# A graph layer's pair work begins five slots behind its split in place of three, with no limit to the tiles planned per slot

## The chip, the core and the metric

The kernel runs on one core of a Trainium2 chip. The core has five engines with instruction streams of their own, each in order: TensorE (PE; its weight loads are listed as PEld), VectorE (DVE), ScalarE (ACT), GpSimd (POOL) and SyncE (SP). They meet through semaphores. DMA transfers run beside them; in this kernel SP issues nearly all plain transfers, and POOL issues the indirect ones.

The metric is the time of one execution on the device in microseconds (us).

## The reference

One message-passing layer over a graph of 6250 nodes and 100000 edges, with rows of 128 numbers, followed by a residual layer norm. The edges come sorted by `dst`.

```python
msg_in = jnp.concatenate([x[src], x[dst], edge_attr], axis=-1)
h = msg_in @ W + b
mu = jnp.mean(h, axis=-1, keepdims=True)
var = jnp.mean(jnp.square(h - mu), axis=-1, keepdims=True)
h = (h - mu) * jax.lax.rsqrt(var + 1e-5) * gamma + beta
msg = jax.nn.relu(h)
out = jax.ops.segment_sum(msg, src, num_segments=6250)
return _layernorm(x + out)
```

## The kernel before

**Two halves and a sort between them.** Edges are taken in 782 tiles of 128, four tiles to a *slot*, 196 slots. The first half of the work handles edges in the order in which they come: `edges(s, q)` (L619, L623) multiplies the four tiles of slot q by the edge part of W and adds, by a product with a one-hot matrix (`edge_hot`, L607), the `dst` node's part from a small window of a node table. `evict` (L633, ACT) copies the result from PSUM to a buffer of the ring `hs`. POOL then scatters each tile's 128 rows to DRAM (L650, `scatters`), to a place that sorts the edges by blocks of `src` nodes. The places are worked out beside this by `places` (L451 to L524, on DVE, PE and ACT), piece by piece, up to about slot 176.

The second half takes the sorted rows back. They lie in *pairs* of node blocks, 25 pairs to a split. `load_pairs` (L725, SP) loads one pair; `ones` (L748, DVE) makes a one-hot matrix of it, `turn` and `turned` (L760 PE, L764 ACT) turn it, `seed` (L770, ACT) and `pick` (L787, PE) add the `src` node's part, `square` (L796, L799, ACT) makes the variance, `root` and `scale` (L805, L811, DVE) normalise, `sums` (L820, PE) sums the messages per node, and `add` (L826, DVE) adds them to the accumulator. The last split is not done by pairs but by `Unit`s at the end, with the final norm.

**Splits.** The edges are cut into six splits that end at slots 42, 84, 126, 156, 176 and 196. A pair of a split can be loaded only when every scatter of that split has landed. A pair of splits 0 to 2 has eight tiles of rows, one of split 3 six, one of split 4 four. In split 4 the first eight *items* hold two pairs each (`TWINS`); all other items hold one pair. There are 117 items.

**The planner.** An item takes four steps; a step runs, in the order of `FLOW`, one stage each of several items, so that items overlap. An item's load stands six steps ahead of its `ones` and twenty ahead of its `add`. The list `due` says at which slot each split's items start and so, by straight lines between, how many steps each slot gets (`steps_due`). In the loop over slots the code of slot q issues, in order: the loads of the edge rows (`eT`, L141), of `db` (L581) and of the window (`win`, L593) for slots up to q + 4; `edges(s, q)`; one step of pair work; `evict(s, q)`; pieces of `places`; the remaining steps; and the scatters of the slot before.

**What holds the streams to each other.** SP is one queue: what stands behind a load that waits is not issued either. The ring `hs` has nine slots' room in three tiles of three slots each; ACT fills the column of block numbers for three slots at once (`fill`, L568, every third slot), and this instruction waits until the scatters of the three slots that had the tile before have landed. Scatters are tied to products on PE (`TIE`), so that POOL spreads them over the next slot.

**Numbers of the planner.** `LAG = 3` starts a split's items three slots behind its end. `MOST = 6.6` keeps the next split from starting before the present one could be done at 6.6 tiles a slot.

Of the kernel before, what the change touches and what calls it, by code (L numbers as in the profile page):

```python
# [22 lines left out]
TILES = 782  # L23
LAST = E - (TILES - 1) * P
NB, BN = 50, 125
RUN = 8
NPAD = 6400
PT = 4
# [9 lines left out]
SPLITS = [(168, 4, 320, [12, 24, 44, 44, 44]),  # L38
          (168, 4, 320, [42, 42, 42, 42]),
          (168, 4, 320, [42, 42, 42, 42]),  # L40
          (120, 3, 192, [40, 40, 40]),
          (80, 2, 128, [40, 40]),
          (78, 2, 128, [39, 39])]
# [15 lines left out]
def first_tiles():  # L59
    out = [0]  # L60
    for n, _, _, _ in SPLITS:
        out.append(out[-1] + n)
    assert out[-1] == TILES
    return out
# [20 lines left out]
def fast_path(ctx, tc, io, bad_d, found):  # L85
# [4 lines left out]
    first_tile = first_tiles()  # L90
# [882 lines left out]
    n_split = len(SPLITS)  # L973
# [95 lines left out]
    TWINS = 8  # L1069
    pairs, first_item = [], []  # L1070
# [50 lines left out]
            n_steps += 1  # L1121

    LEAD, ENDQ, ENDS = 6, 1, 0
    LAG = 3
    MOST = 6.6

    due = []
    for s in range(1, n_split):
        q = first_tile[s] // PT + LAG
        if due:  # L1130
            q = max(q, due[-1][0] + int(NB * SPLITS[s - 2][1] / MOST))
        due.append((q, 4 * first_item[s - 1]))
    q, at0 = due[-1]
    due.append((q + int(4 * TWINS * SPLITS[-2][1] / MOST), at0 + 4 * TWINS))
    due.append((-(-TILES // PT) + ENDQ, len(pairs) * 4 + ENDS))

    def steps_due(q):
# [16 lines left out]
    for s, (n_tiles, _, _, _) in enumerate(SPLITS):  # L1154
        p0, p1 = first_tile[s] // PT, -(-first_tile[s + 1] // PT)
        slots = p1 - p0
        for i in range(slots):
            q = p0 + i
# [140 lines left out]
@with_exitstack  # L1299
def gnn_resnorm_kernel(ctx, tc, io):  # L1300
    nc = tc.nc
    keep = ctx.enter_context(tc.tile_pool(name="keep", bufs=1))
    bad_t = keep.tile([1, 1], I32, name="bad_t")
    with ExitStack() as inner:
        found = []
        fast_path(inner, tc, io, bad_t, found)
    with tc.If(found[0] > 0, preferred_fallthrough_block=True, label="general"):
        with ExitStack() as inner:
            general_path(inner, tc, io)
# [233 lines left out]
```

## Time and profile before

| | |
|---|---|
| runs | 1121.99, 1122.06, 1118.9 us; median 1121.99 |
| the profiled execution | 1117.85 us, its span 1115.9 us |
| PE, DVE busy | 870.6 us (78%), 846.7 us (76%) |
| ACT, POOL busy | 751.9 us (67%), 795.9 us (71%) |
| scatters (L650) | 782 in 757.5 us, from 20.0 to 1023 us |
| DMA | 247.19 MB, 222 GB/s over the span |

An engine's share is an average over very different stretches. A row of the groups gives a line's operation, its count, its busy time and the mean of one, and then the idle time ahead of it with what ended it. A row of the waits names the engine and line that waited, then the one that ended the wait, the sum, the number of waits and the longest. A row of the timeline gives the start, the time taken, the engine, the line, and in brackets the idle time before it with its end. A row of a stretch gives its bounds and length, each engine's busy time with the count of instructions in brackets, then the clock granted to TensorE as a share of full speed, the DMA share and the GB/s; asked for one line, it counts that line alone.

Times in a trace are from the start of the span. The 133rd eviction is slot 132's, since slots count from 0.

### The profile page before, as it was taken

The page shows a single profiled execution, that of the slowest core. Times are in us where ns is not written, and L with a number is a line of the kernel's source. Part 1 is how long each engine was busy: PE and PEld are TensorE (multiplying, and loading weights), DVE is VectorE, ACT ScalarE, POOL GpSimd, SP SyncE. Part 2 cuts the span into 40 slices and gives each one's busy share as a digit, 9 for nine tenths or more (in the row PEclk, how much of TensorE's full clock was granted, in tenths as well). Part 3 has the DMA queues.
Part 4 walks back from the last instruction along what each step waited for, and adds up shares of the span by engine and source line. Part 5 has one row for each costly group of instructions (what it writes and reads, how often), then busy time and mean ns, then how long its engine had stood idle before and what let it go on. Part 6 is the DMA issues. An engine that isn't in the chain of part 4 may idle for free. (4 is left out here: it accounts for less than half of the span.)

```text
span 1115.9 us, 27253 instructions
## 1 busy us (share of the span) xinstructions
PE 870.6 (78%) x8886; PEld 805.4 (72%) x8886; DVE 846.7 (76%) x2368; ACT 751.9 (67%) x2980; POOL 795.9 (71%) x830
## 2 busy tenths in 40 slices
PE   6748755456878888598968678988989899987994
PEld 4647645456867887587868668888878788886773
DVE  8784556628769586688877668889898988877897
ACT  4324422126666667577777657898888899987895
POOL 2777777777777777777777777777777767774254
PEclk7879878668989788898989897999999999999998
DMA  7899999458777763877867648787778767844341
GB/s 216 262 267 272 283 311 284 150 182 286 230 228 253 234 205 126 270 231 245 274 223 242 186 134 281 244 253 241 230 245 259 226 209 241 262 136 141 105 134 61
DMA packets 128049, 247.19 MB, mean 222 GB/s; under 512 B 47005, under 2 KB 61231, under 8 KB 127897
## 3 DMA queue, kind: packets, MB, share of 16 engines
q1 hardware_dynamic: 101924, 191.92, 56.9%
q0 software_dynamic: 25104, 53.05, 13.2%
q8 instruction: 71, 1.16, 0.5%
q14 instruction: 80, 0.66, 0.2%
q10 hardware_dynamic: 870, 0.40, 0.1%
HBM read 155.49 MB, written 89.80 MB: 220 GB/s over the span
## 5 line engine op out<-in xcount | busy, mean ns | idle before, releaser
L650 POOL DMA_INDIRECT sorted<-hs,place_i x782 | 757.5, 969 | 249.8 <-issue 100.9
L787 PE MATMUL sel<-xa,ohn 128*128 128x128 bf16 x2550 | 188.9, 226 | 83.7 <-ACT sel L770 82.0
L619 PEld LDWEIGHTS hp<-w,eT 128*128 128x128 f32 x1564 | 216.4, 212 | 48.7 <-issue 30.2
L820 PE MATMUL pa<-msg,ohe 128*128 128x130 f32 x1700 | 236.6, 292 | 17.1 <-DVE acc L826 8.6
L619 PE MATMUL hp<-w,eT 128*128 128x128 f32 x1564 | 237.7, 300 | 14.1 <-ACT hs L633 14.1
L811 DVE SCALAR_TENSOR_TENSOR msg<-sel,rstd,cut 128x128 f32<-128x128 f32 x850 | 240.6, 345 | 8.0
L796 ACT ACTIVATE sq<-sel 128x128 f32<-128x128 f32 x850 | 223.7, 282 | 23.1 <-PE sel L787 23.1
L787 PEld LDWEIGHTS <-ohn 128*128 128x128 bf16 x2550 | 165.7, 101 | 94.3 <-issue 80.2
L820 PEld LDWEIGHTS pa<-msg,ohe 128*128 128x128 f32 x1700 | 213.9, 201 | 23.2 <-DVE acc L826 10.4
L796 ACT ACTIVATION_READ_ACCUMULATOR sq<-sel 128x1 f32 x850 | 180.9, 213 | 0.0
L748 DVE TENSOR_TENSOR ohe<-hl,beside 128x1024 f32<-128x1024 f32 (+2 forms) x117 | 130.2, 1113 | 57.2 <-DMA hl<-sorted 41.1
L633 ACT COPY hs<-hp 128x512 f32<-128x512 f32 x196 | 113.2, 579 | 59.1 <-PE hp L623 56.7
L770 ACT COPY sel<-hl 128x512 f32<-128x512 f32 (+1 forms) x225 | 128.1, 569 | 33.0 <-DVE msg L811 32.7
L764 ACT COPY ohn<-tr 128x1024 bf16<-128x1024 bf16 (+2 forms) x117 | 107.7, 921 | 5.3 <-PE tr L760 5.3
L607 DVE TENSOR_SCALAR ohd<-db,part_w 128x512 bf16<-128x512 bf16 x192 | 70.4, 367 | 51.7 <-DMA db<-drel_d 48.6
L568 ACT COPY hs<-sloc 128x12 f32<-128x12 f32 x66 | 14.1, 213 | 132.9 <-DMA sorted<-hs,place_i 131.1
L826 DVE TENSOR_TENSOR acc<-acc,pa 128x260 f32<-128x260 f32 x125 | 52.3, 418 | 57.6 <-PE pa L820 56.7
L760 PE MATMUL tr<-ident_h,ohe 128*128 128x128 bf16 x850 | 70.5, 227 | 26.8 <-DVE ohe L748 14.9
L623 PE MATMUL hp<-win,ohd 126*128 126x128 bf16 x782 | 80.8, 228 | 2.3 <-DMA win<-xb_d 2.3
L805 DVE RECIPROCAL rstd<-std 128x4 f32<-128x4 f32 (+1 forms) x225 | 38.1, 169 | 57.7 <-ACT std L799 56.0
L760 PEld LDWEIGHTS <-ohe 128*128 128x128 bf16 x850 | 55.6, 102 | 28.0 <-DVE ohe L748 16.1
L799 ACT ACTIVATE std<-ss,eps 128x4 f32<-128x4 f32 (+1 forms) x225 | 66.9, 297 | 7.3
(198 smaller groups left out, 1039.3 us busy)
## 6 DMA issues: line engine op xcount, KB each, us to landing
eT<-in_eT SPq DMA_DIRECT2D x96, 512.0 KB
hl<-sorted SPq DMA_DIRECT2D x75, 528.0 KB
db<-drel_d SPq DMA_DIRECT2D x96, 256.0 KB
sorted<-empty SPq DMA_DIRECT2D x100, 198.0 KB
hl<-sorted SPq DMA_DIRECT2D x50, 264.0 KB
sorted<-hs,place_i POOLq DMA_INDIRECT x782
hl<-sorted SPq DMA_DIRECT2D x25, 396.0 KB
sorted<-empty SPq DMA_DIRECT2D x50, 132.0 KB
```

The lines of the kernel that those rows point to most:

```text
L619: pe(nc.tensor.matmul(hp[:, j, :], eT[:, at], w[:, 2, :], start=j == 0, stop=False, skip_group_check=True), 4)
L623: pe(nc.tensor.matmul(hp[:, j, :], oh[:3 * WN, at], win[:3 * WN, :], start=False, stop=j == m - 1, skip_group_check=True))
L633: nc.scalar.copy(hs[:, :m, 0:D], hp[:, :m, :])
L650: i = nc.gpsimd.indirect_dma_start(out=sorted_d[s][:, :], out_offset=bass.IndirectOffsetOnAxis(ap=place_i[:parts, t:t + 1], axis=0), in_=h ...
L748: nc.vector.tensor_tensor(self.ohe[:, :k, :], self.hl[:, :k, D:D + 1].to_broadcast([P, k, P]), row_bc(iota_p, k), op=ALU.is_equal)
L760: pe(nc.tensor.transpose(tr[:, j, :], half[:, j0 + j, 1::2], ident_h))
L764: nc.scalar.copy(self.ohn[:, :self.k, :], self.tr[:, :self.k, :])
L770: nc.scalar.copy(self.sel[g][:, :m, :], self.hl[:, j0:j0 + m, 0:D])
L787: pe(nc.tensor.matmul(sel[:, j, :], self.ohn[:, j0 + j, :], xa[:, b, i * D:(i + 1) * D], start=False, stop=j == m - 1 and i == 2, skip_gro ...
L796: nc.scalar.activation(sq[:, j, :], self.sel[g][:, j, :], AF.Square, accum_out=ss[:, j:j + 1])
L811: nc.vector.scalar_tensor_tensor(self.msg[:, j0 + j, 0:D], self.sel[g][:, j, :], rstd[:, j:j + 1], cut, op0=ALU.mult, op1=ALU.max)
L820: pe(nc.tensor.matmul(self.pa[:, h, :], self.ohe[:, i * k + j, :], self.msg[:, i * k + j, :], start=(j == h), stop=(j == k - 2 + h)), 4)
```

## The change

`LAG` becomes 5, `MOST` goes, and the start of a split's items no longer looks at the split before. The date at which the two-pair items end is reckoned by another formula.

```diff
     LEAD, ENDQ, ENDS = 6, 1, 0
-    LAG = 3
-    MOST = 6.6
-
-    due = []
-    for s in range(1, n_split):
-        q = first_tile[s] // PT + LAG
-        if due:
-            q = max(q, due[-1][0] + int(NB * SPLITS[s - 2][1] / MOST))
-        due.append((q, 4 * first_item[s - 1]))
+    LAG = 5
+
+    due = [(first_tile[s] // PT + LAG, 4 * first_item[s - 1]) for s in range(1, n_split)]
     q, at0 = due[-1]
-    due.append((q + int(4 * TWINS * SPLITS[-2][1] / MOST), at0 + 4 * TWINS))
+    due.append((q + (TILES // PT + ENDQ - q) * 2 * TWINS // (NB // 2), at0 + 4 * TWINS))
     due.append((-(-TILES // PT) + ENDQ, len(pairs) * 4 + ENDS))
```

Worked out, the list of dates is this (slot at which the items begin):

| items of | steps counted there | before | after |
|---|---|---|---|
| split 0 | 0 | 45 | 47 |
| split 1 | 100 | 87 | 89 |
| split 2 | 200 | 129 | 131 |
| split 3 | 300 | 159 | 161 |
| split 4, two-pair items | 400 | 181 | 181 |
| split 4, single items | 432 | 190 | 190 |
| end | 468 | 197 | 197 |

Splits 0, 1 and 2 have the same number of slots as before (42, 42, 30). Split 3 has 20 in place of 22: five steps a slot for 4.5, and 25 pairs of six tiles in 20 slots are 7.5 tiles a slot for 6.8. In the list of before the limit moved one date, split 4's, from 179 to 181.

ACT at the boundary of split 2, before: the rows around `fill` of slot 132 (L568, `hs2_195`). `hl_8429` is the last pair of split 1, `hl_8566` the first of split 2.

```order
L770 COPY sel_8793<-hl_8429 128x512
L796 ACTIVATE sq_8796,ss_8795<-sel_8752 128x128 x4
L799 ACTIVATE std_8801<-ss_8795,eps_100 128x4
L764 COPY ohn_8775<-tr_8776 128x1024
L568 COPY hs2_195<-sloc_164 128x12
L633 COPY hs2_195<-hp_8819 128x4x128
L770 COPY sel_8867<-hl_8566 128x512
```

The same place in the changed kernel; `hl_8373` and `hl_8492` are the last two pairs of split 1.

```order
L568 COPY hs2_195<-sloc_164 128x12
L633 COPY hs2_195<-hp_8672 128x4x128
L770 COPY sel_8746<-hl_8373 128x512
L796 ACTIVATE sq_8749,ss_8748<-sel_8696 128x128 x4
L799 ACTIVATE std_8754<-ss_8748,eps_100 128x4
L764 COPY ohn_8728<-tr_8729 128x1024
L633 COPY hs2_195<-hp_8768 128x4x128
L477 ACTIVATE sc_8465<-sc_8465 128x1000
L770 COPY sel_8813<-hl_8492 128x512
```

Before, split 1's last pair is seeded ahead of slot 132's `fill`, and the first pair of split 2 follows the eviction; now the last two pairs of split 1 are still seeded behind that `fill` and two evictions, and split 2's first pair comes two slots later. On SP, 134 window loads stand ahead of the first load of split 2 before, and 136 now.

ACT in slot 167, in the stage of split 3, from its eviction to the `fill` of slot 168, before:

```order
L633 COPY hs_194<-hp 128x4x128
L770 COPY sel<-hl 128x384
L796 ACTIVATE sq,ss<-sel 128x128 x3
L799 ACTIVATE std<-ss,eps 128x3
L764 COPY ohn<-tr 128x768
L770 COPY sel<-hl 128x384
L796 ACTIVATE sq,ss<-sel 128x128 x3
L799 ACTIVATE std<-ss,eps 128x3
L568 COPY hs_195<-sloc 128x12
```

And in the changed kernel:

```order
L633 COPY hs_194<-hp 128x4x128
L770 COPY sel<-hl 128x384
L796 ACTIVATE sq,ss<-sel 128x128 x3
L799 ACTIVATE std<-ss,eps 128x3
L770 COPY sel<-hl 128x384
L796 ACTIVATE sq,ss<-sel 128x128 x3
L799 ACTIVATE std<-ss,eps 128x3
L764 COPY ohn<-tr 128x768
L770 COPY sel<-hl 128x384
L796 ACTIVATE sq,ss<-sel 128x128 x3
L799 ACTIVATE std<-ss,eps 128x3
L568 COPY hs_195<-sloc 128x12
```

One more group of seed, squares and root stands between the two evictions.

## The prediction

> **What bounds the kernel now.** I read the groups of the page first, then the waits of ACT and of SP's queue, then the timeline where the longest waits stand, and last a ledger by stage. The groups and waits:
>
> ```profile
> L650 POOL DMA_INDIRECT sorted<-hs,place_i x782 | 757.5, 969 | 249.8 <-issue 100.9
> ACT hs L568 <- DMA sorted<-hs,place_i: 131.1, 27, 11.1
> ```
>
> POOL issues one scatter after the other, with 0.3 us between them, and ACT waits 27 times, 131.1 us in all, for a buffer of the ring `hs` that POOL has not yet emptied: over much of the program POOL sets the pace. Whether it does so everywhere is told by counting evictions (L633, one a slot), scatters (L650) and finished pairs (L826) in the same stretches:
>
> ```profile
> 236.50:660.00 423.50, 48.45 (x84) 0.89 0.72 228
> 236.50:660.00 423.50, 322.23 (x333) 0.89 0.72 228
> 0.00:676.50 676.50, 77.05 (x133) 0.85 0.75 234
> 676.50:820.30 143.80, 15.58 (x27) 0.98 0.77 243
> 826.50:918.50 92.00, 9.24 (x16) 1.00 0.75 230
> 676.50:820.30 143.80, 109.33 (x114) 0.98 0.77 243
> 826.50:918.50 92.00, 66.06 (x69) 1.00 0.75 230
> ```
>
> (Each row: the stretch, its length, busy time and count, then clock, DMA share and GB/s. Rows 1, 3, 4 and 5 are evictions, rows 2, 6 and 7 scatters.) From 236.5 to 660 us, 84 slots take 423.5 us, 5.04 a slot, and 333 scatters take 1.27 us each, four of them 5.09: POOL's pace. From 676.5 to 820.3 a slot takes 143.8/27 = 5.33, more than POOL needs, and from 826.5 to 918.5 it takes 92/16 = 5.75. There POOL runs dry: 69 scatters at 1.27 are 87.6 of 92 us, so 4.4 us are lost. So from the eviction of slot 132 (the 133rd, in at 676.5) the other engines are the bound, and they are evenly full:
>
> ```profile
> 676.50:820.30 143.80, 128.12 (x1491) 122.86 (x1490) 125.77 (x356) 125.15 (x515) 109.33 (x114) 0.98 0.77 243
> 826.50:918.50 92.00, 80.72 (x936) 76.19 (x934) 81.56 (x241) 82.69 (x348) 66.06 (x69) 1.00 0.75 230
> 918.50:942.50 24.00, 22.30 (x265) 21.25 (x265) 20.86 (x71) 23.39 (x102) 18.21 (x20) 1.00 0.76 236
> ```
>
> PE, DVE and ACT stand at 87 to 90% in the first two rows (PE, its weight loads, DVE, ACT, POOL). What comes ahead of 676.5 is a stall, where split 2's first pair is loaded (waits of SP's queue, then timeline rows of SP, DVE, ACT and PE):
>
> ```profile
> SPq L725 <- DMA sorted<-hs,place_i: 30.0, 1, 30.0
> SPq L725 <- DMA sorted<-hs,place_i: 18.0, 1, 18.0
> SPq L725 <- DMA sorted<-hs,place_i: 19.1, 1, 19.1
> SPq L725 <- DMA sorted<-hs,place_i: 3.4, 1, 3.4
> 664.17 0.34 SPq L725 DMA_DIRECT2D hl<-sorted  x1
> 668.27 1.22 DVE L748 TENSOR_TENSOR ohe<-hl,beside 128x1024 f32<-128x1024 f32 x1 [7.81 <-DMA hl<-sorted]
> 672.96 0.59 ACT L770 COPY sel<-hl 128x512 f32<-128x512 f32 x1 [10.74 <-DVE msg L811]
> 675.85 0.59 ACT L633 COPY hs<-hp 128x512 f32<-128x512 f32 x1
> 669.55 1.03 PE L760 MATMUL tr<-ident_h,ohe 128*128 128x128 bf16 x8 [7.50 <-DVE ohe L748]
> ```
>
> The four waits are the ends of splits 0 to 3. At the third the load leaves at 664.17, when the last scatter of slot 125 has landed; DVE stands for 7.81 us, PE 7.50, ACT 10.74. After the first two stalls the slots are light enough to make the loss good at POOL's pace; after the third they never do, as every slot costs more than 5.09.
>
> **The change part by part.** Due times of splits 0 to 3 move two slots later; 181, 190 and 197 stay. Nothing is added or removed: 117 items, 782 scatters, the same loads.
>
> *Splits 0 and 1.* Evictions wait for POOL there and POOL keeps its 5.09 a slot throughout, stalls of 30.0 and 18.0 us included. Cost zero, hidden by POOL's backlog; without it each later pair would cost its whole time.
>
> *The third boundary.* The same loads and edges now stand two slots further on when SP comes to the first load of split 2: 136 window loads are ahead of it in place of 134. The release stays at 664.17, since POOL sets it. Two estimates give the moment that answers to 676.4, the end of slot 132's eviction, which is now the end of slot 134's. From the load: 676.4 again, at most, as DVE's first `ohe` can begin at 668.27. From the ring: slot 132's buffer (L568, every third slot) wants slots 123 to 125 landed, the same event, so its eviction ends about 664.2 + 0.6 = 664.8, and two slots at 5.33 make 675.5. I take 676.0, with -1 and +2 as ends: **-0.4 us**.
>
> *From there to slot 181.* Before: 143.8 to slot 159, 6.2 to slot 160, 92.0 to slot 176, 24.0 to slot 181, in all 266.0 us for 49 slots; the finished pairs in them are
>
> ```profile
> 676.50:820.30 143.80, 9.59 (x23) 0.98 0.77 243
> 820.30:826.50 6.20, 0.41 (x1) 1.00 0.97 317
> 826.50:918.50 92.00, 7.49 (x18) 1.00 0.75 230
> 918.50:942.50 24.00, 2.50 (x6) 1.00 0.76 236
> ```
>
> 48. After: the same 48 in 47 slots. So two slots of edges without pairs leave the bounded stretch. PE's part of one is these rows, 1.11 + 0.39 = 1.50 us:
>
> ```profile
> 681.70 1.11 PE L619 MATMUL hp<-w,eT 128*128 128x128 f32 x8
> 682.64 0.39 PE L623 MATMUL hp<-win,ohd 126*128 126x128 bf16 x4
> 88.60:104.20 15.60, 3.58 (x6) 1.00 0.92 278
> ```
>
> At the 88% to which PE is filled that is 1.7 us a slot, so **-3.4 us** for two. Below: ACT's eviction alone (0.58 us at 90%), 1.3 for two. Above: the quickest run of slots without pairs, six evictions in 15.6 us (last row), 2.6 a slot, 5.2 for two.
>
> *The denser stage.* Split 3's 25 pairs take 20 slots in place of 22: 7.5 tiles a slot for 6.8, five steps a slot for 4.5. If time goes by work, slots 161 to 181 take 266.0 - 143.8 - 3.4 = 118.8 us, 5.94 each, against 5.09 for POOL. The lead over POOL pays for that. At its own pace POOL lands slot 161 at 664.2 + 36 x 5.09 = 847.4; the slot is evicted at 676.0 + 143.8 = 819.8, so the lead is 27.6 us. Before, slot 160 led by only 842.4 - 826.5 = 15.9 when POOL began to run dry. At 5.94 - 5.09 = 0.85 a slot, 20 slots eat 17 us, and POOL runs dry in the last few slots before 181 at most. Cost beyond the ledger: zero, if no engine waits longer per step; it is the thinnest part.
>
> *From slot 181.* Same due times, same items, same units behind; PE, DVE and ACT bring their gain along, and POOL, which no longer loses the 4.4 us, comes as early.
>
> Sum: -0.4 - 3.4 = **-3.8 us**. The profiled execution took 1117.85 us with a span of 1115.9; that becomes 1114.0 and 1112.1. The median of the runs, 1121.99, lies 4.1 above the profiled execution, so I forecast 1118.2 for a median.
>
> *The clock.* A stall also halves PE's clock; the same 16 products before and after the stall, and a short wait at slot 123:
>
> ```profile
> 653.83 2.00 PE L820 MATMUL pa<-msg,ohe 128*128 128x130 f32 x16
> 676.38 3.82 PE L820 MATMUL pa<-msg,ohe 128*128 128x130 f32 x16
> 620.77 0.21 ACT L568 COPY hs<-sloc 128x12 f32<-128x12 f32 x1 [5.39 <-DMA sorted<-hs,place_i]
> 622.91 1.22 PE L787 MATMUL sel<-xa,ohn 128*128 128x128 bf16 x12 [2.63 <-ACT sel L770]
> 624.78 1.98 PE L619 MATMUL hp<-w,eT 128*128 128x128 f32 x8
> 664.00:668.00 4.00, 0.00 (x0) 0.00 (x0) 0.00 (x0) 0.00 (x0) 2.95 (x4) 0.52 0.73 194
> ```
>
> After the long stall L820 costs 1.8 us more; after a wait of 2.63 us L619 still costs 0.9 more (1.98 for 1.11). The change swaps a long stall for a wait on the ring like that at 620.77, so the halving stays, only shorter. The Trainium skill, TensorE: Matmul & The Clock Gate, section HAM oscillation — how this bites in real kernels, says that gaps over about 3.4 us throttle the array again. By it a wait of 2.63 us should cost nothing, and the change would save the whole slow stretch; the trace shows slow products behind that wait, so the row decides here. I leave this term out of the sum and make it a rival.
>
> **The rivals.**
>
> (a) *The dense stage gets slower steps.* Place: slots 161 to 181, DVE and ACT. For it: both are at 89 and 90% in the row of 826.5, and a fifth step in a slot finds no slack. Against it: ACT reaches 39.68 of 41.0 us (97%) at the two-pair items:
>
> ```profile
> 942.50:983.50 41.00, 36.74 (x438) 35.54 (x438) 32.62 (x98) 39.68 (x169) 31.25 (x33) 1.00 0.81 255
> 840.00:860.00 20.00, 17.57 (x205) 16.55 (x205) 15.87 (x50) 17.37 (x73) 14.51 (x15) 1.00 0.76 239
> ```
>
> It decides from (942.4 - 819.8)/20 = 6.13 us a slot: above that slot 181 is later than before, and POOL dry for it. If DVE is held at the 79% of its worst 20 us (second row) in place of 89%, 118.8 becomes 133.8, 11 us later than before; half way, 6.5 a slot, is +7: **1129**.
>
> (b) *The ring takes the stall's place.* Slot 135 wants the buffers of slots 126 to 128, so evictions can meet the ring's end there and at slot 138, and the two slots gained are waited away. For it: the 131.1 us of L568. Against: slot 128 has landed at 664.2 + 3 x 5.09 = 679.4, and slot 135 comes at 676.0 + 5.3 = 681.3. Then the gain is 0 to 1: **1121.5**.
>
> (c) *The clock comes back too.* L820 1.8 us, L787 1.2, L619 0.9 and the rest of the slow stretch to 681 are about 4.6 us, against 1.8 behind a short wait; were all 2.8 on the path, **1115.4**.
>
> (d) That the change does nothing it says is out: the orders differ at every boundary. Only the limit on tiles is nearly idle: it held back split 4 alone, and its new date is the same 181.
>
> **How the numbers follow.** Forecast 0.45, its own range 1115.5 to 1120; (a) 0.30, (b) 0.13, (c) 0.12. A measurement of this kernel tells about 0.3%, 3.4 us, from no change. The forecast is barely past that: 0.33 of its 0.45 faster, 0.12 same. (c) is faster, (b) same, (a) slower but for 0.04. Faster 0.45, same 0.29, slower 0.26. The range leaves out 0.1 at each end: above most of (a), below a gain of both ledger ends with the clock: 1111 to 1128.
>
> **What would show it.** At the third boundary SP's wait of 19.1 us falls to about 9, and DVE's of 7.81 to under 3; ACT's total at L568 grows by 10 us or more. Slot 134 is evicted at 676, slot 161 near 820, slot 181 near 938.6; POOL's scatters from 826.5 to 918.5 are 72, not 69. Wrong: slots 161 to 181 take over 122 us (a); evictions 135 to 140 wait at L568 (b); or everything holds to 181 and the gain is lost behind it, which I have no row for.

## The result, and the profile after

Over 17 runs each, taken in turn on the same chips, the changed kernel has a median of 1116.76 us (1114.78 to 1119.06) and the kernel before 1119.7 us (1117.3 to 1123.26). The ratio is 0.9967, with a 95% interval of 0.9959 to 0.9976: 3.7 us of 1120, or 0.33%.

The runs of one kernel spread over some 5 us, more than the effect. The profiled execution of before, at 1117.85, is one of its quicker ones; that of the changed kernel, at 1116.76, is its median. So the two traces show how the time is spent, but their ends lie only 1.0 us apart (spans 1115.9 and 1114.9).

SP's waits at the ends of splits 0 to 3 in the changed kernel:

```profile
SPq L725 <- DMA sorted<-hs,place_i: 18.6, 1, 18.6
SPq L725 <- DMA sorted<-hs,place_i: 13.0, 1, 13.0
SPq L725 <- DMA sorted<-hs,place_i: 14.2, 1, 14.2
SPq L725 <- DMA sorted<-hs,place_i: 3.8, 1, 3.8
```

The first three were 30.0, 18.0 and 19.1. At the third, DVE, which had stood for 7.81 us, now stands for 2.46 (timeline of DVE):

```profile
669.87 1.22 DVE L748 TENSOR_TENSOR ohe<-hl,beside 128x1024 f32<-128x1024 f32 x1 [2.46 <-DMA hl<-sorted]
```

The load itself left at 665.85 us, where it had left at 664.17 (timeline of SP):

```profile
665.85 0.34 SPq L725 DMA_DIRECT2D hl<-sorted  x1
```

What stands in the stall's place is the ring (timeline of ACT, then of PE, then ACT's waits over the whole program):

```profile
653.12 0.21 ACT L568 COPY hs<-sloc 128x12 f32<-128x12 f32 x1 [4.06 <-DMA sorted<-hs,place_i]
665.82 0.21 ACT L568 COPY hs<-sloc 128x12 f32<-128x12 f32 x1 [0.74 <-DMA sorted<-hs,place_i]
```

```profile
654.35 1.25 PE L787 MATMUL sel<-xa,ohn 128*128 128x128 bf16 x12 [3.29 <-ACT sel L770]
655.39 3.27 PE L820 MATMUL pa<-msg,ohe 128*128 128x130 f32 x16
662.78 2.00 PE L820 MATMUL pa<-msg,ohe 128*128 128x130 f32 x16
668.63 2.01 PE L820 MATMUL pa<-msg,ohe 128*128 128x130 f32 x16
```

```profile
ACT hs L568 <- DMA sorted<-hs,place_i: 157.0, 33, 14.9
```

ACT waits 4.06 us at slot 129's fill and 0.74 at slot 132's; from 640 to 690 us it waits there 6.6 us in all, and in the kernel before not at all. PE's products are slow from 654 to 658.5 and at full pace after that, where before they were slow from 669.5 to 681.

The stages behind the boundary, cut at the evictions of slots 134, 161 and 181 (first evictions, L633, then finished pairs, L826, then all engines: PE, its weight loads, DVE, ACT, POOL):

```profile
0.00:677.80 677.80, 78.19 (x135) 0.85 0.75 235
677.80:823.40 145.60, 15.64 (x27) 0.98 0.77 246
823.40:941.30 117.90, 11.55 (x20) 1.00 0.71 229
```

```profile
677.80:823.40 145.60, 9.57 (x23) 0.98 0.77 246
823.40:941.30 117.90, 10.41 (x25) 1.00 0.71 229
```

```profile
677.80:823.40 145.60, 127.04 (x1472) 121.40 (x1472) 127.40 (x356) 124.68 (x514) 110.85 (x115) 0.98 0.77 246
823.40:941.30 117.90, 105.01 (x1235) 99.57 (x1232) 104.79 (x320) 109.83 (x469) 88.24 (x92) 1.00 0.71 229
```

Slot 134 is evicted at 677.8, where the kernel before had done slot 132 at 676.5. So the evictions are further ahead of POOL, and this distance is called the lead from here on: the time from the end of a slot's eviction to the start of its last scatter. At slot 134 it is 707.7 - 687.9 = 19.8 us before and 708.1 - 677.7 = 30.4 after, at slot 161 10.9 and 22.6. Slots 161 to 181 cost 117.9/20 = 5.90 us each with five steps in each; ACT is the fullest there, with 109.83/117.9 = 93%.

POOL's scatters from 826.5 to 941.5 us, the stretch of split 3, in the kernel before and in the changed one:

```profile
826.50:941.50 115.00, 83.57 (x87) 1.00 0.76 232
```

```profile
826.50:941.50 115.00, 86.05 (x89) 1.00 0.71 229
```

At 1.27 us a scatter POOL could issue 115/1.27 = 90.5; where it issues fewer it stands *dry*, without a slot to scatter. The first and the last scatter's start, before and after:

```profile
L650 POOL DMA_INDIRECT sorted<-hs,place_i x782: 868/967/1178, 20.0 to 1022.9; - x196
```

```profile
L650 POOL DMA_INDIRECT sorted<-hs,place_i x782: 867/967/1482, 19.6 to 1021.7; - x196
```

From the last scatter's start to the end it is 1115.9 - 1022.9 = 93.0 and 1114.9 - 1021.7 = 93.2 us. This is the reading that orders the runs below: in eight of the eleven profiles of the next table this tail is 93.0 to 93.4 us. There a kernel's time is the moment of POOL's last scatter plus the tail, and that moment is POOL's own pace plus what POOL stands dry: 782 scatters begin 781 steps apart, 781 x 1.272 = 993.4 us, and before it is 20.0 + 993.4 + 9.5 us of standing dry.

### The profile page after: what moved, and what is told of

Its sections match the earlier page's. It is cut to its first block, busy times and chain, and to the rows that moved or that the text cites. A ratio compares the mean times of both kernels' runs of the same rounds, so it can differ in the third digit from the quotient of the medians.

```text
span 1114.9 us, 27250 instructions
## 1 busy us (share of the span) xinstructions
PE 872.9 (78%) x8886; PEld 807.9 (72%) x8886; DVE 845.3 (76%) x2368; ACT 752.4 (67%) x2980; POOL 797.5 (72%) x830
## 5 line engine op out<-in xcount | busy, mean ns | idle before, releaser
L619 PE MATMUL hp<-w,eT 128*128 128x128 f32 x1564 | 240.5, 303 | 20.8 <-ACT hs L633 20.8
L796 ACT ACTIVATE sq<-sel 128x128 f32<-128x128 f32 x850 | 223.6, 282 | 30.6 <-PE sel L787 30.4
L820 PE MATMUL pa<-msg,ohe 128*128 128x130 f32 x1700 | 231.8, 289 | 15.3 <-DVE acc L826 8.6
L820 PEld LDWEIGHTS pa<-msg,ohe 128*128 128x128 f32 x1700 | 211.4, 200 | 19.8 <-DVE acc L826 10.3
L748 DVE TENSOR_TENSOR ohe<-hl,beside 128x1024 f32<-128x1024 f32 (+2 forms) x117 | 130.2, 1113 | 21.9 <-DMA hl<-sorted 11.6
L633 ACT COPY hs<-hp 128x512 f32<-128x512 f32 x196 | 113.3, 579 | 42.8 <-PE hp L623 40.1
L770 ACT COPY sel<-hl 128x512 f32<-128x512 f32 (+1 forms) x225 | 128.1, 570 | 13.6 <-DVE msg L811 13.2
L568 ACT COPY hs<-sloc 128x12 f32<-128x12 f32 x66 | 14.1, 213 | 159.8 <-DMA sorted<-hs,place_i 157.0
L826 DVE TENSOR_TENSOR acc<-acc,pa 128x260 f32<-128x260 f32 x125 | 52.3, 418 | 58.8 <-PE pa L820 58.7
L623 PEld LDWEIGHTS <-ohd 126*128 126x128 bf16 x782 | 66.4, 105 | 6.0 <-issue 2.4
```

The lines of the kernel that those rows point to most:

```text
L619: pe(nc.tensor.matmul(hp[:, j, :], eT[:, at], w[:, 2, :], start=j == 0, stop=False, skip_group_check=True), 4)
L623: pe(nc.tensor.matmul(hp[:, j, :], oh[:3 * WN, at], win[:3 * WN, :], start=False, stop=j == m - 1, skip_group_check=True))
L633: nc.scalar.copy(hs[:, :m, 0:D], hp[:, :m, :])
L748: nc.vector.tensor_tensor(self.ohe[:, :k, :], self.hl[:, :k, D:D + 1].to_broadcast([P, k, P]), row_bc(iota_p, k), op=ALU.is_equal)
L770: nc.scalar.copy(self.sel[g][:, :m, :], self.hl[:, j0:j0 + m, 0:D])
L796: nc.scalar.activation(sq[:, j, :], self.sel[g][:, j, :], AF.Square, accum_out=ss[:, j:j + 1])
```

## The experiments

Each kernel was timed beside the kernel before, on the same chip. Three kernels that were timed on a chip where every kernel is slower are left out of this table; they come below. The ratios, and what the profiles show. The last two columns are worked out from the starts of the scatters in each trace: what the time from the first scatter of slot 160 to the first of slot 181 exceeds 84 x 1.272 us, and the time from there to the last scatter 57 x 1.272:

| kernel | ratio to before, 95% interval | last scatter begins | span | tail | scatters in 826.5 to 941.5 | dry, slots 160 to 180 | dry, from 181 |
|---|---|---|---|---|---|---|---|
| before | 1 | 1022.9 | 1115.9 | 93.0 | 87 | 5.3 | 1.9 |
| changed | 0.9967 (0.9959 to 0.9976) | 1021.7 | 1114.9 | 93.2 | 89 | 2.0 | 3.3 |
| late_third | 0.9964 (0.9952 to 0.9976) | 1020.1 | 1113.1 | 93.0 | 90 | 0.7 | 3.3 |
| late_first_two | 1.0007 (0.9995 to 1.0019) | 1025.8 | 1118.9 | 93.1 | 85 | 7.8 | 1.9 |
| only_split2 | 0.9959 (0.9945 to 0.9973) | 1023.3 | 1117.4 | 94.1 | 89 | 3.0 | 1.9 |
| no_limit | 1.0069 (1.0056 to 1.0083) | 1031.5 | 1126.8 | 95.3 | 80 | 14.7 | 0.0 |
| lag5_limit | 0.9963 (0.9948 to 0.9979) | 1016.1 | 1113.7 | 97.6 | 91 | 0.2 | 0.2 |
| lag7 | 1.0087 (1.0065 to 1.0109) | 1035.3 | 1128.4 | 93.1 | 86 | 7.1 | 12.4 |
| dense18_b | 1.0073 (1.0055 to 1.0092) | 1032.9 | 1126.1 | 93.2 | 83 | 12.4 | 3.4 |
| ring12_lag5 | 0.9950 (0.9934 to 0.9966) | 1017.5 | 1110.9 | 93.4 | 91 | 0.0 | 2.8 |
| ring12_lag8 | 0.9952 (0.9936 to 0.9968) | 1019.5 | 1112.7 | 93.2 | 90 | 0.3 | 1.6 |

(only_split2's profiled execution, 1119.18 us, is the slowest of its five; its median is 1116.39. POOL stood dry for 4.3 us in its first 44 slots, where its dates are those of the kernel before, which lost 1.6 there.)

The runs of one kernel differ by as much as the effect, as that one shows, but the dry time from slot 160 on goes with the date of split 2's boundary. With 131 it is 5.3, 4.0 and 4.9 us (changed, late_third, only_split2), with 129 it is 7.2 and 9.7 (before, late_first_two). The means are 3.7 us apart, as much as the ratio.

### Which boundary carries the gain

late_third moves the dates of splits 2 and 3 alone, late_first_two those of splits 0 and 1 alone, only_split2 that of split 2 alone:

```diff
-    due = [(first_tile[s] // PT + LAG, 4 * first_item[s - 1]) for s in range(1, n_split)]
+    due = [(first_tile[s] // PT + LAG[s], 4 * first_item[s - 1]) for s in range(1, n_split)]
 # late_third
+    LAG = {1: 3, 2: 3, 3: 5, 4: 5, 5: 5}
 # late_first_two
+    LAG = {1: 5, 2: 5, 3: 3, 4: 3, 5: 5}
 # only_split2
+    LAG = {1: 3, 2: 3, 3: 5, 4: 3, 5: 5}
```

> Splits 2 and 3 begin five slots behind their end, as in the changed kernel (131, 161), splits 0 and 1 three, as before (45, 87); split 4 at 181. Stall theory (two slots of edges move out of the bounded stretch at the boundary of split 2): the whole gain, a ratio to before of 0.9965 to 0.9975, SP's wait there 10 to 15 us, and slot 134 evicted near 677 us. Early theory (the gain comes from the boundaries of splits 0 and 1): 1.000. Chance theory (it comes from how the steps of the places meet those of the pairs, which any shift stirs up): anywhere from 0.995 to 1.003.

> Splits 0 and 1 begin five slots behind their end (47, 89), splits 2 and 3 three, as before (129, 159); split 4 at 181. Stall theory: no gain, 0.9995 to 1.001, as the stall of 19 us on SP at split 2's boundary stays and POOL hides the other two. Early theory: the whole gain, 0.9967.

> Only split 2 begins two slots later (131); split 3 stays at 159, so split 2's items have 28 slots in place of 30, 7.1 tiles a slot, and split 3's 22. Stall theory: the whole gain again, 0.9965 to 0.9975, since the work behind the stall is the same in another order. Lead theory (it takes split 3's later start too, since the edges must stay ahead of POOL): half of it or less, 0.998 to 1.000.

Measured: 0.9964, 1.0007 and 0.9959. In late_third SP's wait there is 12.1 us and slot 134 is evicted at 676.7, both as the stall theory had it. The whole gain sits at split 2's boundary, and one date, 129 to 131, is enough for it. The early theory falls: with splits 0 and 1 moved the interval holds 1 and not 0.9967. The chance theory is not needed: three kernels that share the one date, and differ in the others, agree within their intervals, and the one without it has none of the gain. The lead theory, which asked for split 3's later start too, falls as well.

### The limit alone

```diff
-    LAG = 5
+    LAG = 3
```

> Three slots behind, as before, with the limit on tiles taken away alone: the dates are 45, 87, 129, 159 and then 179 for split 4 (181 before), 189 for its single items. Stall theory: nothing, 0.999 to 1.001; the stall at split 2 is as before, and the work behind it is the same in all. If the denser split 3 (20 slots) costs time in itself: slower, 1.002 or more.

Measured: 1.0069, so slower by 0.7% where I had expected nothing. The limit's formula for the two-pair items goes with it, which moves the single items from 190 to 189. Split 3 is as dense as in the changed kernel, five steps a slot, but the evictions have not gained on POOL at split 2's boundary: at slot 134 the lead is 708.6 - 688.6 = 20.0 us, as before. POOL's row over the same stretch as above:

```profile
826.50:941.50 115.00, 76.30 (x80) 0.99 0.70 224
```

80 scatters in place of 87, so 7 x 1.27 = 9 us more in which POOL stands dry, and its last scatter begins 8.6 us later (1031.5 for 1022.9). The pairs that were done early there bring nothing back, for the end waits for POOL. So taking the limit away costs 0.7% at three slots, while with five slots the pair of edits gains 0.3%.

### The later start with the limit kept

```diff
-    LAG = 3
+    LAG = 5
```

(made in the kernel before, so that the dates are 47, 89, 131, 161, 183, 192)

> Five slots behind, but the limit of 6.6 tiles a slot and its formulas kept: dates 47, 89, 131, 161, then 183 for split 4 (the limit binds: 161 + 22) and 192 for its single items, which have five slots in place of seven. Lead theory (a stage may be dense only while the evictions are far ahead of POOL's scatters; POOL's lost time is not made good): split 3 is a little lighter, but the single items' 36 steps in five slots, 7.2 a slot, come when the lead is gone, so POOL runs dry at slots 192 to 196 by 5 us or more: 0.999 to 1.003. Theory that the limit does nothing once the boundary is at five slots: 0.9967 as the changed kernel.

Measured: 0.9963. The first theory's number was wrong. POOL is not dry at the end: split 3 in 22 slots keeps enough of the lead to carry the single items.

```profile
826.50:941.50 115.00, 87.55 (x91) 1.00 0.76 235
941.50:1016.50 75.00, 57.02 (x60) 1.00 0.59 181
```

Both rows are at full pace (115/91 = 1.26, 75/60 = 1.25), and the last scatter begins 5.6 us sooner than in the changed kernel. Yet the time is the same: the tail grows from 93.2 to 97.6 us, since more work is left when POOL is through: PE is busy for 79.99 us from 1017 to 1113, and in the changed kernel for 76.33 from 1022 to 1114. With five slots, then, taking the limit away costs nothing that these runs can tell (0.9967 beside 0.9963); it only moves work between these two places.

### Seven slots

```diff
-    LAG = 5
+    LAG = 7
```

> Seven slots behind in place of five: dates 49, 91, 133, 163, 181. Ring theory (evictions can be at most about seven to nine slots ahead of POOL, so two further slots of edges can't be put into the stall; ACT waits at the ring in their place, and split 3 has 18 slots, 8.3 tiles each): no better than five, 0.997 to 1.002, with SP's wait at split 2's boundary gone and ACT's total at the ring's fill above 170 us. Stall theory without a ring: another 3 us, 0.994.

Measured: 1.0087. The expectation has the dates wrong: seven slots move split 4 as well, to 183, so split 3 keeps 20 slots and the two-pair items and the single items are pressed into eight and six slots. The trace shows both parts. At split 2's boundary the load finds its rows all but landed (SP's waits) and ACT waits at the ring (ACT's waits, both between the boundary's bounds of 640 and 690 us; 179.7 in all):

```profile
SPq L725 <- DMA sorted<-hs,place_i: 1.1, 1, 1.1
```

```profile
ACT hs L568 <- DMA sorted<-hs,place_i: 13.5, 3, 7.3
```

And POOL issues 61 scatters from 945 to 1035 us, where 90/1.27 = 71 were possible:

```profile
945.00:1035.00 90.00, 58.76 (x61) 1.00 0.58 175
```

So the ring theory's direction holds, that two further slots bring nothing, but its price was read from the wrong dates. The last scatter begins 13.6 us later than in the changed kernel. POOL stands dry for 5.1 us more in slots 160 to 180, and for 9.1 us more from slot 181 on, where the items are pressed. So the larger part is the end's; how much of the other the ring at the boundary costs is open.

### Density with a lead

Split 3 in 18 slots, all else as in the changed kernel:

```diff
-    LAG = 5
+    LAG = {1: 5, 2: 5, 3: 5, 4: 7, 5: 5}
```

> Dates 47, 89, 131, then 163 for split 3 (161 in the changed kernel), 181: split 2 has 32 slots, split 3 only 18, 8.3 tiles a slot. Lead theory (a dense stage costs nothing while the evictions lead POOL by more than the stage eats; the time is POOL's last scatter plus 92 us): the lead at slot 163 is larger than before by what split 2 saves, the work up to slot 181 is the same, POOL dry for 1 to 4 us between slots 160 and 182: 0.996 to 0.998. Theory that density costs time in itself: 0.999 or more.

On that chip every kernel took about 1350 us, the one before included: 0.9987 (0.9965 to 1.0009). In this trace POOL has gaps of up to 3.6 us for no reason that the trace names, so nothing of the kernel's own balance can be read there. The same kernel on a chip of the usual speed:

> The same kernel as dense18 once more (dates 47, 89, 131, 163, 181; split 3 in 18 slots, 8.3 tiles a slot), since that job ran where all kernels, the one before included, took 1350 us. Lead theory: 0.996 to 0.998, POOL dry for 1 to 4 us between slots 160 and 182, last scatter plus 92 us. Theory that density costs time in itself: 0.999 or more.

Measured: 1.0073. The lead theory's number was wrong. Evictions, then finished pairs, from the eviction of slot 134 to those of slots 161 and 181:

```profile
677.90:823.80 145.90, 15.56 (x27) 0.96 0.77 245
823.80:952.50 128.70, 11.58 (x20) 0.98 0.69 212
```

```profile
677.90:823.80 145.90, 8.75 (x21) 0.96 0.77 245
823.80:952.50 128.70, 11.27 (x27) 0.98 0.69 212
```

The first stretch has 21 pairs in place of 23 and takes 145.9 us in place of 145.6: by these two traces, lighter slots are not quicker there. Of the time that should have been saved 1.5 us went into a longer wait at the ring (3.3 us for 1.8), and the granted clock was 0.96 for 0.98; the rest is not explained. The engines are less full in it (all engines of this kernel; DVE 123.02 of 145.9, 84%, where the changed kernel has 127.40 of 145.6, 87%):

```profile
677.90:823.80 145.90, 122.16 (x1390) 117.44 (x1389) 123.02 (x339) 118.08 (x483) 110.82 (x116) 0.96 0.77 245
823.80:952.50 128.70, 114.97 (x1323) 109.30 (x1322) 111.31 (x337) 117.61 (x501) 88.80 (x92) 0.98 0.69 212
```

So no lead is gained by putting two pairs off (23.1 us at slot 161, for 22.6), and the two pairs cost 128.7 - 117.9 = 10.8 us in the next stage. POOL stands dry for 12.4 us there in place of 2.0. This is the price of density: not per step (128.7/27 = 4.8 us a pair against 117.9/25 = 4.7), but as slots that run longer than POOL's four scatters and eat the lead.

### A larger ring

Twelve slots in `hs` in place of nine. To make room `w3`, `iota_row`, `sgn` and `b_bc` go to the pool that closes at slot 44, and the scratch tile of the squares has one buffer (the diff leaves out the four moved tiles, and two further places like that of `sq`):

```diff
-    HS, HG = 9, 3
+    HS, HG = 12, 3
-            sq = blk.tile([P, PT, P], F32, name="sq")
+            sq = blk.tile([P, PT, P], F32, name="sq", bufs=1)
 # ring12_lag8, beside this
+    LAG = {1: 8, 2: 8, 3: 8, 4: 8, 5: 5}
```

> The ring has twelve slots in place of nine (some early tiles go to the pool that closes at slot 44, and the scratch of the squares has one buffer in place of two, to make room), and splits 0 to 3 begin eight slots behind: 50, 92, 134, 164; split 4 at 181. Ring theory: three more slots of edges go ahead of split 2's boundary, 3 x 1.7 = 5 us less behind it, POOL never runs dry up to slot 181: 0.991 to 0.994, lead at slot 137 above 35 us. Theory that five slots is the best for another reason (a later split 3 is too dense: 17 slots, 8.8 tiles each): 0.997 or more.

> The ring of twelve slots alone, dates as in the changed kernel. Ring theory: the order of work is that of the changed kernel, and at split 2's boundary the load is waited for again in place of the ring: 0.996 to 0.998. If the ring's waits cost time by themselves anywhere else (ACT waits 157 us there in the changed kernel): 0.994 or less.

> The ring of twelve slots with the dates of the kernel before (three slots, limit kept). Queue theory (at three slots it is SP, stopped at the first load of a split with the edges' loads behind it, that holds the edges, not the ring): the stall of split 2 keeps its place in the program, so nothing is gained there; 0.9985 to 1.0005. Ring theory alone (more buffers, more lead): 0.995 as with five slots.

> The ring of twelve slots and six slots behind for splits 0 to 3 (48, 90, 132, 162), split 4 at 181. If the time is POOL's last scatter plus 92 us, and POOL is dry for only some 5 us of the whole run with the twelve slots and five: the floor is near, 0.993 to 0.995, at best 2 us under that kernel. If the moved edges count in full (1.7 us a slot): 0.9935.

Measured: 0.9952 with eight slots, 0.9950 with five; each ratio lies between the numbers of its two theories, so neither number held. ring12_lag3 and ring12_lag6 were timed only on the chip on which every kernel took 1350 us (0.9998, 0.9972 to 1.0025; and 0.9972, 0.9948 to 0.9996) and tell nothing of this balance. In the kernel before ACT does not wait at the ring at all from 640 to 690 us; whether a larger ring would help at three slots is left open all the same. With twelve slots and five behind, the wait for the load is back (waits between 640 and 690, ring12_lag5):

```profile
DVE ohe L748 <- DMA hl<-sorted: 17.8, 1, 17.8
```

and still the kernel is no slower for it: POOL's backlog hides the stall (the lead at slot 134 is 31.4 us), POOL keeps its pace through split 3 (91 scatters, dry for 0.0 us), and the tail is 93.4. Three more slots of edges in that stall (ring12_lag8) buy nothing further: the lead at slot 161 grows from 25.4 to 38.1 us, but POOL was not dry before slot 181 any more, so there was nothing left to save there. My 5 us for them did not come. ring12_lag5 has the lowest median of all, 1114.71 us, and is quicker than the kernel before; from the changed kernel its interval does not separate it.

## Why the prediction was right, and where its steps were not

**What bounds the kernel.** Right, and it reaches further than I put it. From slot 132 the other engines are slower than POOL, and from about slot 160, when the lead is eaten, POOL runs dry; and because most of these kernels end 93 us after POOL's last scatter, dry time there is what the kernel pays. no_limit and dense18_b show it with the sign turned round.

**Splits 0 and 1 at zero.** Right: late_first_two, 1.0007.

**The third boundary, -0.4.** Slot 134 came at 677.8, not 676.0: +1.3 against the 676.5 of before, inside the ends of -1 and +2. The step that was off is "The release stays at 664.17": the load left at 665.85, 1.7 us later. In the traces of eight of these kernels it left between 664.02 and 666.96, so the figure of one trace was taken for a fixed one. From the release to the eviction it is 11.9 us, for 12.3 before: 0.4 less, as forecast. The ring bound where I had put it, at slot 132 (0.74 us), and also at slot 129 (4.06 us), where I had not. The load bound less: DVE stood 2.46 us for it, and in late_third, only_split2 and lag5_limit not at all.

**The work behind it, -3.4.** The sum nearly held: 145.6 + 117.9 = 263.5 us against 262.6 forecast and 266.0 before, so 2.5 us were saved. Its ground did not quite. I priced two slots of edges by PE's share, as if time went by work. dense18_b shows a stretch in which two pairs less save nothing, so 1.7 us a slot is not shown as the price of an edge slot, and 2.5 for 3.4 may be chance. Shown is that the date at split 2's boundary alone brings the whole 0.3 to 0.4%.

**The size.** -3.8 us forecast. By the ratio it is -3.7; by the two profiles slot 181 came at 941.3 for 942.5, 1.2 us sooner and not 3.8. The profile of before is a quick one of its kernel, which is part of that difference; how much of it, one trace of each cannot say. That the two sizes agree to 0.1 us is luck: the interval alone goes from 2.7 to 4.6 us, and the terms were off in both directions. One was missing, too: I had POOL lose next to nothing any more. It still lost 2.0 us in slots 160 to 180 (5.3 before), and from slot 181 on it lost more, 3.3 for 1.9. As a time, 1118.2 was forecast and 1116.76 measured; the kernel before, from which it was reckoned, had a median of 1121.99 in three runs and of 1119.7 in 17.

**The denser stage and rival (a).** 118.8 us forecast for slots 161 to 181, 117.9 measured; 5.90 us a slot, under the 6.13 from which (a) would have decided. The lead that was to pay for it was smaller than I had it: slot 161 was evicted at 823.4, not 819.8, which takes 3.6 us off the 27.6. The rival's price is real all the same: at 128.7/20 = 6.4 a slot the median of dense18_b is 1128.46 beside 1120.96, 7.5 us more, where I had priced (a) at +7 for 6.5 a slot. That price was not what I called it: half way between 118.8 and 133.8 us are 6.3 a slot and +4 us, not 6.5 and +7. And the rival's mechanism, slower steps, is not what dense18_b shows: DVE does not fall to 79% (it is at 111.31/128.7 = 86%), a pair costs 4.8 us for 4.7, and there are more steps in each slot than the lead can pay for.

**Rival (d) and the limit.** Here a sentence was wrong: "Only the limit on tiles is nearly idle". It moved split 4's date by two slots, and with its formula the single items' by one, and that is worth 0.7% as long as the start is at three.

**Rival (b).** The ring did take part of the stall's place, with 4.8 us at slots 129 and 132, but at slots 135 and 138, where I had put it, next to nothing: one wait of 1.8 us in all from 677.8 to 823.4. ACT's total at L568 went from 131.1 to 157.0, more than the 10 us that I had named as a sign, but only 6.6 of these 25.9 us lie at split 2's boundary; the others come earlier, so the total is no sign of what happens there.

**The clock and rival (c).** I said that the halving stays, only shorter. So it was: four microseconds behind the ring's wait in place of twelve. L820 took 3.27 us in place of 2.00 behind a gap of 3.29, at a granted clock of 0.82 from 652 to 656 us and 0.75 from 656 to 660. By the page of the Trainium skill on the clock gate (TensorE: Matmul & The Clock Gate, section HAM oscillation — how this bites in real kernels) a gap has to exceed about 3.4 us. The trace shows that a gap just under that is enough, and the 2.63 us of the kernel before were too; the measurement decides. How much of the gain is the clock's was not tried alone.

**The signs.** Scatters from 826.5 to 918.5 were 71, where I forecast 72 and before had 69 (POOL of the changed kernel):

```profile
826.50:918.50 92.00, 68.92 (x71) 1.00 0.71 229
```

SP's third wait fell to 14.2, not to 9: 1.7 us of that are the later release, and SP came to the load of split 2 some 3.5 us sooner than I had reckoned from the evictions. In late_third it fell to 12.1, in only_split2 to 9.7. DVE's wait fell to 2.46, under the 3 forecast.

## What to carry to other kernels

When one engine's queue sets the end, ask of every edit what it does to the lead over that queue: work put into a wait lengthens the lead, a dense stage eats it, and what the queue stands dry is never made good. An edit can cost time alone and nothing beside another, as taking the limit away did here, so run each alone before giving either the credit. And in a pipeline whose engines wait for each other, a slot with less work need not be a shorter slot, as one pair of traces showed here: price by measured slots, not by shares.

## What the hardware showed that I had not expected

A gap of 3.29 us on PE, less than half the 7.50 us of before, was enough to slow the 16 products behind it from 2.00 to 3.27 us (all engines of the changed kernel; the granted clock is the first figure behind the counts):

```profile
652.00:656.00 4.00, 1.65 (x15) 1.65 (x15) 3.83 (x6) 2.85 (x13) 3.06 (x4) 0.82 0.39 118
656.00:660.00 4.00, 4.00 (x34) 3.99 (x34) 2.63 (x7) 3.12 (x13) 3.08 (x4) 0.75 0.15 51
```

And on one chip, not that of the other experiments, all four kernels that were timed took some 20% longer (1353 us for the kernel before), at a mean granted clock of 0.85 in place of 0.90 and with waits on POOL that the trace puts down to nothing; why, these runs do not show (dense18, then the changed kernel):

```profile
POOL sorted L650 <- issue: 197.3, 520, 3.6
```

```profile
POOL sorted L650 <- issue: 100.0, 328, 0.3
```
